# Search for the largest scores in layer 3's attention: four heads at a time on row quarters of TensorE, PSUM banks split four and two

## The chip, the cores and the metric

The kernel runs on one core of a Trainium2 chip. The core has five engines that the profile lists: TensorE (PE for its matmuls, PEld for its weight loads), VectorE (DVE), ScalarE (ACT), GpSimd (POOL) and SyncE (SP, which here only issues transfers). They run side by side, each works through its own queue in order, and semaphores tie them together. Matmuls write to PSUM, which has 8 banks of 512 float32 per partition; VectorE and ScalarE read it from there.

The metric is the device time of one execution, in microseconds (us). The kernel before takes 12436.45 us, the median of three runs (12427.92 to 12447.01).

## The reference

The program is a chain of four layers on a batch of 4 images with 128 channels and 48 x 48 = 2304 positions: a selective-scan block, a deformable convolution, a linear-attention transformer with a mixture of experts, and causal softmax attention with a second mixture of experts. Only the attention of the last layer is touched:

```python
qkv = jnp.einsum('btc,oc->bto', x, qkv_w) + qkv_b
q, k, v = jnp.split(qkv, 3, axis=-1)
q, k, v = (heads(q), heads(k), heads(v))      # 4 heads of 32
scale = 1.0 / np.sqrt(HEAD_DIM)
att = jnp.einsum('bhqd,bhkd->bhqk', q, k) * scale
att = jnp.where(causal, att, -jnp.inf)
att = jax.nn.softmax(att, axis=-1)
out = jnp.einsum('bhqk,bhkd->bhqd', att, v)
out = out.transpose(0, 2, 1, 3).reshape(B, T, C)
return jnp.einsum('btc,oc->bto', out, out_w) + out_b
```

All is float32, x is layer-normalised before it, and the result is added to the stream.

## The kernel before

**Tiling.** An image's 2304 positions are 18 tiles of 128, and 6 blocks (`j`) of three tiles, 384 queries each. The four heads are worked as two pairs (`p`, NP3 = 2). `q` and `k` lie transposed, [128 rows, pair, 2304]: a pair's first head has rows 0 to 31, its second rows 64 to 95. Rows 32 and 96 of `k` hold 1.0, and the same rows of `q` are to receive minus the largest score of each query, so that the score matmul over 64 rows yields score minus maximum and the exponential needs no further pass.

**Two passes over the scores.** The first is the search (`largest`, L2039). For a query tile `i` and a slice `s` of up to 512 keys, one *part* makes the scores of one pair: two matmuls (L2052), one for each head on 64 rows of the array, into the two banks of the tile `sc`. VectorE adds the causal mask in the last slice of a query tile (L2061), reduces over the keys (L2062), and after the last slice takes the maximum over slices (L2065) and writes its negative into `spread` (L2066). When a block's parts are done, `take` turns `spread` by three transposes (L2071) into the tile `ps` and adds it to `q` (L2073). `sc` has one buffer, so a part's matmuls wait for the reduction of the part before.

The second pass goes by *units*, one for each block, pair and key tile `t` up to the diagonal: `scores` (L2105) makes the transposed scores of 128 keys and up to 384 queries for both heads into the two banks of `scT`, ScalarE exponentiates them (L2113) into `pT`, GpSimd zeroes the future on diagonal tiles (L2116), and `weighed` (L2134) multiplies by the values and accumulates into `out`. `scT` has two buffers, so the next unit's scores can be written while the exponential reads the last. There are 4 images x 2 pairs x (3 + 6 + 9 + 12 + 15 + 18) = 504 units, and 4 x 2 x 50 = 400 parts, of which 288 span 512 keys, 32 span 384, 40 span 256 and 40 span 128. A float32 matmul shows in the trace as two matmul and two weight-load records.

**PSUM.** `ps` (projections, transposes and all else) has 1 bank, `sc` 2, `scT` 2 x 2, `out` 1: all 8.

**Order.** The instruction order of each engine is that of the program text. While block `x` = (image, j, p) is worked, the parts of the *following* block (the other pair, or the next j, or the next image) are spread over its units. Other work is popped one step at a time: `others` (normalising, transposing and projecting later blocks and the next image, every second unit, or every unit in blocks under 7 units) and `doing` (dividing by the sums, output projection). `weighed` runs three units behind `scores` (UNIT_LAG). So TensorE's order in a unit is

```python
scores(x, t)
while parts and (total - len(parts)) * max(n - 1, 1) < total * (t + 1):
    parts.pop(0)()
if doing:
    doing.pop(0)()
if others and (t % 2 == 0 or n < 7):
    others.pop(0)()
```

and then `weighed` of an earlier unit. At the end of each block `take` runs. The weights' layout, which puts each head on its rows, is made on the host in `layout`.

Of the kernel before, what the change touches and what calls it, by code (L numbers as in the profile page):

```python
# [15 lines left out]
F32 = mybir.dt.float32  # L16
# [3 lines left out]
AX = mybir.AxisListType  # L20
PSUM = bass.MemoryType.PSUM
DRAM = bass.MemoryType.DRAM

P = 128
NB = 4
C = 128
HW = 48
L = HW * HW
NT = L // P
BLK = 384  # L30
NBLK = L // BLK
G3 = BLK // P
# [33 lines left out]
DH3 = C // NH3  # L66
NP3 = NH3 // 2
# [1840 lines left out]
        _layer3(ctx, env, io, T)  # L1908


UNIT_LAG = 3


def _layer3(ctx, env, io, T):
# [6 lines left out]
    nc, tc, ident = env.nc, env.tc, env.ident  # L1921
    cp = ctx.enter_context(tc.tile_pool(name="l3c", bufs=1))
    bp = ctx.enter_context(tc.tile_pool(name="l3b", bufs=2))
    sp = ctx.enter_context(tc.tile_pool(name="l3s", bufs=2))
    ps = ctx.enter_context(tc.tile_pool(name="l3p", bufs=1, space=PSUM))
    pa = ctx.enter_context(tc.tile_pool(name="l3a", bufs=1, space=PSUM))
    pb = ctx.enter_context(tc.tile_pool(name="l3x", bufs=2, space=PSUM))
    po = ctx.enter_context(tc.tile_pool(name="l3o", bufs=1, space=PSUM))

    def load(name, shape):  # L1930
        t = cp.tile(shape, F32, name=name)
        nc.sync.dma_start(t, io[name])
        return t

    def psum(*shape):
        return ps.tile(list(shape), F32, name="ps", tag="ps")

    w_qk = load("l3_wqk", [P, 2, NP3, P])
    b_qk = load("l3_bqk", [P, 2, NP3])
# [5 lines left out]
    later = load("l3_later", [P, P])  # L1945

    spread = [cp.tile([P, G3, P], F32, name=f"spread{i}") for i in range(NP3)]
# [11 lines left out]
    def normed(im):  # L1959

        t = {}

        def some(g0):
            if g0 == 0:
                t["st"] = sp.tile([P, NT, nc.vector.BN_STATS_DIM], F32, name="st")
                im.mv = sp.tile([P, NT, nc.vector.BN_AGGR_DIM], F32, name="mv")
                im.rstd = sp.tile([P, NT], F32, name="rstd")
                im.q = bp.tile([P, NP3, L], F32, name="q")
                im.k = bp.tile([P, NP3, L], F32, name="k")
            for g in range(g0, g0 + G3):  # L1970
                nc.vector.bn_stats(out=t["st"][:, g, :], in_=im.T[:, g, :])
                nc.vector.bn_aggr(out=im.mv[:, g, :], in_=t["st"][:, g, :])
            if g0 + G3 == NT:
                nc.vector.tensor_scalar_add(im.rstd, im.mv[:, :, 1], 1e-5)
                nc.gpsimd.tensor_tensor(im.rstd, im.rstd, env.half[:, :NT], ALU.pow)

        return [lambda g0=g0: some(g0) for g0 in range(0, NT, G3)]
# [58 lines left out]
            lambda s=s, p=p: project(s, p) for s in range(2) for p in range(NP3)  # L2036
        ] + [value]

    def largest(im, j, p):  # L2039

        neg = spread[p]
        t = {}

        def part(i, s):
            n = (i + 1) * P
            at, end = s * 512, min(s * 512 + 512, n)
            if s == 0:
                t["mx"] = sp.tile([P, 2, 5], F32, name="mx")
            sc = pa.tile([P, 2, 512], F32, name="sc")
            for r in range(2):  # L2050
                rows = slice(r * 64, r * 64 + 64)
                nc.tensor.matmul(  # L2052
                    sc[:, r, : end - at],
                    im.q[rows, p, bass.ts(i, P)],
                    im.k[rows, p, at:end],
                    start=True,
                    stop=True,
                )
            if end == n:
                own = sc[:, :, n - P - at : n - at]  # L2060
                nc.vector.tensor_add(own, own, later.unsqueeze(1).to_broadcast([P, 2, P]))  # L2061
            nc.vector.reduce_max(t["mx"][:, :, s], sc[:, :, : end - at], axis=AX.X)  # L2062
            if end == n:
                top = sp.tile([P, 2], F32, name="top")
                nc.vector.reduce_max(top, t["mx"][:, :, : s + 1], axis=AX.X)  # L2065
                nc.vector.tensor_scalar_mul(neg[:, i - j * G3, DH3 :: 2 * DH3], top, -1.0)  # L2066

        def take():
            pm = psum(P, BLK)
            for g in range(G3):  # L2070
                nc.tensor.transpose(pm[:, bass.ts(g, P)], neg[:, g, :], ident)  # L2071
            at = bass.ts(j, BLK)
            nc.vector.tensor_add(im.q[:, p, at], im.q[:, p, at], pm)  # L2073

        parts = [
            lambda i=i, s=s: part(i, s)
            for i in range(j * G3, (j + 1) * G3)
            for s in range(-(-(i + 1) * P // 512))
        ]
        return parts, take  # L2080

    def output(im, j, oT):
        def project():
# [15 lines left out]
    def scores(x, t):  # L2099
# [3 lines left out]
        for r in range(2):  # L2103
# [7 lines left out]
            )  # L2111
        pT = sp.tile([P, 2, BLK], F32, name="pT", bufs=UNIT_LAG + 2)
        nc.scalar.activation(pT[:, :, cols], sc[:, :, cols], AF.Exp)  # L2113
# [40 lines left out]
    def divide(x):  # L2154
        oT, den = x.im.sums

        def invert(i):
            part = bass.ts(i, BLK // 2)
            nc.vector.reciprocal(den[:, part], den[:, part])
            if i:  # L2160
                nc.vector.tensor_mul(oT, oT, den)

        wait = lambda: None
        return [
            wait,
            wait,
            lambda: invert(0),
            lambda: invert(1),
            wait,
            output(x.im, x.j, oT),  # L2170
        ]
# [5 lines left out]
    images = [Image(b) for b in range(NB)]  # L2177
    blocks = [Block(im, j, p) for im in images for j in range(NBLK) for p in range(NP3)]

    def preparation(im):  # L2180
        return normed(im) + [s for j in range(NBLK) for s in prepare(im, j)]

    def run(steps):
        for s in steps:
            s()

    with tc.manual_schedule(engines=ORDERED):
        pr = psum(1, C)
        nc.tensor.matmul(pr, v_b, oT_w, start=True, stop=True)
        nc.vector.tensor_add(o_b, o_b, pr)  # L2190
        pr = psum(P, C)
        nc.tensor.matmul(pr, env.ones_row, o_b, start=True, stop=True)
        nc.scalar.copy(bias[:, 0, :], pr)
        run(normed(images[0]) + prepare(images[0], 0))
        parts, take = largest(images[0], 0, 0)
        run(parts + [take])
        others = [s for j in range(1, NBLK) for s in prepare(images[0], j)]
        waiting, done, doing = [], [], []
        for i, x in enumerate(blocks):
            n = x.last + 1  # L2200
            if x.j == 0 and x.p == 0 and x.im.b + 1 < NB:
                others += preparation(images[x.im.b + 1])
            following = blocks[i + 1] if i + 1 < len(blocks) else None
            parts, take = largest(following.im, following.j, following.p) if following else ([], None)
            if following and following.im is x.im and x.im.b == 0:

                need = (NBLK - 1 - following.j) * (2 + 2 * NP3 + 1)
                need += 0 if x.im.b + 1 == NB else len(preparation(images[1]))
                while len(others) > need:
                    others.pop(0)()  # L2210
            total = len(parts)
            for t in range(n):
                scores(x, t)
                while parts and (total - len(parts)) * max(n - 1, 1) < total * (t + 1):
                    parts.pop(0)()
                if doing:
                    doing.pop(0)()
                if others and (t % 2 == 0 or n < 7):
                    others.pop(0)()
                waiting.append((x, t))  # L2220
                if len(waiting) > UNIT_LAG:
                    y, s = waiting.pop(0)
                    weighed(y, s)
                    if s == y.last and y.p == NP3 - 1:
                        doing += divide(y)
            run(parts)
            if following and following.im is not x.im:
                run(others)
                others = []
            if take:  # L2230
                take()
        for y, s in waiting:
            weighed(y, s)
            if s == y.last and y.p == NP3 - 1:
                doing += divide(y)
        run(doing)
# [57 lines left out]
def layout(i):  # L2294
# [12 lines left out]
    l3 = {k[8:]: v for k, v in i.items() if k.startswith("L3_attn_")}  # L2307
# [6 lines left out]
    for h in range(NH2):  # L2314
        proj[:, h * DH2 : (h + 1) * DH2, h * NF : (h + 1) * NF] = l2["proj"].transpose(0, 2, 1)

    w_qk = np.zeros((C, 2, NP3, 2, 2, DH3), np.float32)
    w_qk[:, :, :, :, 0] = l3["qkv_w"][: 2 * C].T.reshape(C, 2, NP3, 2, DH3)
    w_qk = w_qk.reshape(C, 2, NP3, P)
    b_qk = np.zeros((2, NP3, 2, 2, DH3), np.float32)  # L2320
    b_qk[:, :, :, 0] = l3["qkv_b"][: 2 * C].reshape(2, NP3, 2, DH3)
    b_qk[1, :, :, 1, 0] = 1.0
    b_qk = b_qk.reshape(2, NP3, P).transpose(2, 0, 1)
    o = {
        "x": i["x"].reshape(NB, C, L),
# [66 lines left out]
```

## Time and profile before

| what | value |
|---|---|
| median of three runs | 12436.45 us |
| profiled execution, its own time | 12545.34 us |
| its span, first to last instruction | 12543.6 us |
| layer 3's attention in it | about 10908 to 12330 us, 1422 us |
| TensorE busy in that stretch | 1288.85 us |
| VectorE busy in that stretch | 708.59 us |
| ScalarE busy in that stretch | 448.01 us |
| mean granted TensorE clock there / over the span | 0.96 / 0.949 |

The profiled execution is 109 us longer than the median of the unprofiled runs. The attention is 11% of the span. "Busy" is the share of time in which an engine shows an instruction; for matmuls the ends are modelled and neighbours overlap, so the distance between the starts of two groups tells more than a busy time. In a timeline line the first column is the start in us, the second how long the merged group shows, `x4` how many records it merges, and what stands in brackets is how long the engine was idle before it and what ended that.

### The profile page before, as it was taken

The numbers are of one execution on the slowest core, as the hardware profiler recorded it, in microseconds if no ns is written. First come the engines' busy times: TensorE is split into PE (matmuls) and PEld (weight loads), VectorE is DVE, ScalarE is ACT, GpSimd is POOL, SyncE is SP. The second block draws the span as 40 slices with busy tenths as digits, with TensorE's granted clock in tenths as the row PEclk, the third lists the DMA queues.
The fourth block names the chain that finished last, engine by engine and source line by source line (L and its number), as shares of the span: only waits on it lengthen the run. The fifth ranks groups of instructions, "written<-read, shape, count | busy, mean of one in ns | idle before, by whom it ended". The sixth has DMA issues, their size and how long they took to land.

```text
span 12543.6 us, 192625 instructions
## 1 busy us (share of the span) xinstructions
PE 10872.6 (87%) x71008; PEld 8365.3 (67%) x71008; DVE 8487.3 (68%) x15484; ACT 6888.6 (55%) x13190; POOL 4409.7 (35%) x4799
## 2 busy tenths in 40 slices
PE   7788787978887787688879999999999999698897
PEld 6667666766676666588857777777777777333333
DVE  6998989888988899544456656566566565455554
ACT  5777767777777777411135655555556555232332
POOL 2433434333333343366633333333333332100001
PEclk9999999999999999899979999999999999799998
DMA  3221222122212222356500000000000000300003
GB/s 122 68 70 63 80 77 71 63 76 80 70 64 76 79 67 67 111 171 177 170 21 2 4 3 3 4 2 4 2 3 5 1 1 12 115 7 8 8 8 126
DMA packets 329879, 677.51 MB, mean 54 GB/s; under 512 B 41556, under 2 KB 152168, under 8 KB 328048
## 3 DMA queue, kind: packets, MB, share of 16 engines
q1 hardware_dynamic: 276064, 493.50, 12.3%
q0 software_dynamic: 51840, 169.91, 4.8%
q8 instruction: 570, 9.34, 0.3%
q14 instruction: 365, 2.99, 0.1%
q10 hardware_dynamic: 1040, 1.77, 0.0%
HBM read 602.63 MB, written 71.85 MB: 54 GB/s over the span
## 4 chain that ended last, share of the span: by engine, by line
PE 43%; DVE 7%; ACT 3%; issue 1%; DMA 1%; POOL 1%; another core or an unknown queue 0%; SPq 0%; ACTq 0%; DVEq 0%; POOLq 0%
PE psum L1466 4%; PE pt L1003 4%; PE psum L1458 4%; PE pc L1352 3%; PE psum L1402 3%; PE scT L2105 3%; PE sc L2052 3%; PE out L2134 3%; PE psum L1372 2%; PE psum L1212 2%; PE psum L1213 2%; PE psum L1146 2%; PE psum L1290 1%; PE psum L1391 1%; DVE mx L1375 1%
## 5 line engine op out<-in xcount | busy, mean ns | idle before, releaser
L576 ACT ACTIVATE hs<-ps,bct 128x256 f32<-128x256 f32 x4608 | 1853.8, 474 | 1174.9 <-PE ps L570 1122.5
L570 PE MATMUL ps<-ident,h 128*128 128x128 f32 x9216 | 1491.9, 294 | 783.4 <-DVE h L556 612.7
L570 PEld LDWEIGHTS ps<-ident,h 128*128 128x128 f32 x9216 | 1079.7, 148 | 1168.7 <-DVE h L556 720.3
L584 PE MATMUL yp<-ident,hs 128*128 128x128 f32 x9216 | 1399.3, 288 | 28.5 <-ACT ys L599 28.5
L516 ACT ACTIVATE dA<-delta,l_Al 128x768 f32<-128x768 f32 x1536 | 1388.2, 936 | 0.3
L523 POOL TENSOR_TENSOR h<-du,rB 128x512 f32<-128x512 f32 x768 | 1077.5, 1403 | 757.9 <-PE ps L570 683.1
L584 PEld LDWEIGHTS yp<-ident,hs 128*128 128x128 f32 x9216 | 1151.2, 150 | 83.6 <-ACT ys L599 57.6
L556 DVE TENSOR_TENSOR_SCAN h<-dA,h 128x256 f32<-128x256 f32 (+1 forms) x1024 | 1084.4, 1059 | 27.3
L556 DVE TENSOR_TENSOR_SCAN h<-dA,carry,h 128x768 f32<-128x768 f32 x512 | 1027.1, 2006 | 10.5 <-ACT dA L516 10.5
L1206 POOL TENSOR_TENSOR T<-T,bias 128x384 f32<-128x384 f32 x384 | 383.7, 999 | 1563.5 <-DVE fn L1134 1523.2
L498 POOL TENSOR_SCALAR_AFFINE_SELECT dB<-bct 128x512 f32<-128x512 f32 x768 | 746.0, 971 | 358.4 <-PE b L530 240.9
L2113 ACT ACTIVATE pT<-scT 128x768 f32<-128x768 f32 (+2 forms) x504 | 377.6, 749 | 841.0 <-PE scT L2105 838.9
L530 PE MATMUL b<-dB,duT 128*128 128x128 f32 x6144 | 828.3, 279 | 0.8 <-ACT duT L456 0.8
L556 DVE TENSOR_TENSOR_SCAN h<-dA,carry,b 128x512 f32<-128x512 f32 x512 | 645.7, 1261 | 263.1 <-PE b L530 242.7
L1003 PE MATMUL pt<-ident,gw 128*128 128x128 f32 x5184 | 685.1, 294 | 147.2 <-DVE gw L997 117.6
L990 POOL DMA_INDIRECT g<-table,idx x648 | 659.9, 1018 | 390.0 <-DVE gw L997 189.6
L530 PEld LDWEIGHTS b<-dB,duT 128*128 128x128 f32 x6144 | 768.6, 196 | 2.4 <-POOL h L523 1.2
L1003 PEld LDWEIGHTS pt<-ident,gw 128*128 128x128 f32 x5184 | 650.1, 207 | 176.9 <-DVE gw L997 110.6
L997 DVE TENSOR_TENSOR gw<-g,wq 128x512 f32<-128x512 f32 x648 | 428.7, 692 | 496.9 <-PE pt L1003 416.7
L563 POOL COPY carry<-h 128x2 f32<-128x2 f32 x512 | 96.8, 189 | 1782.0 <-DVE h L556 1717.7
L2062 DVE TENSOR_REDUCE mx<-sc 128x2 f32<-128x1024 f32 (+3 forms) x400 | 428.3, 1071 | 345.2 <-PE sc L2052 340.2
L527 DVE TENSOR_TENSOR h<-du,rB 128x512 f32<-128x512 f32 x768 | 638.7, 832 | 1.6 <-DMA rB<-rows 1.4
(394 smaller groups left out, 22833.0 us busy)
## 6 DMA issues: line engine op xcount, KB each, us to landing
rB<-rows SPq DMA_DIRECT2D x768, 384.0 KB
w<-f_w SPq DMA_DIRECT2D x64, 1024.0 KB
table<-zero SPq DMA_DIRECT2D x162, 128.0 KB
table<-tok SPq DMA_DIRECT2D x16, 1152.0 KB
g<-table,idx POOLq DMA_INDIRECT x648
yd<-y SPq DMA_DIRECT2D x4, 2304.0 KB
sums<-raw SPq DMA_DIRECT2D x192, 48.0 KB
xb<-x SPq DMA_DIRECT2D x42, 192.0 KB
```

Of the source, the lines that this page charges most:

```text
L498: nc.gpsimd.affine_select(out=x.dB[n], in_=x.bc[:, m0 : m0 + CT // P, n : n + 1].to_broadcast([P, CT // P, P]), pattern=[[0, CT // P], [1, ...
L516: nc.scalar.activation(dA, x.delta[:, d, :], AF.Exp, scale=A[:, d, x.k, n : n + 1])
L523: nc.gpsimd.tensor_mul(h[:, 1, own], x.du[:, 1, own], x.rB[n][:, own])
L527: nc.vector.tensor_mul(x.h[n][:, :, own], x.du[:, :, own], b)
L530: nc.tensor.matmul(b0[:, bass.ts(m, P)], x.duT[:, m, :], x.dB[n][:, m, :], start=True, stop=True,)
L556: nc.vector.tensor_tensor_scan(h, da, b, initial=first, op0=ALU.mult, op1=ALU.add)
L570: nc.tensor.transpose(tt[:, m, bass.ts(d, P)], x.h[n][:, d, bass.ts(2 * q + m, P)], ident)
L576: nc.scalar.activation(hs, tt[:, m, :], AF.Copy, scale=x.bc[:, 2 * q + m, NS + n : NS + n + 1])
L584: nc.tensor.matmul(yp[:, q, (2 * d + m) * P : (2 * d + m + 1) * P], hs[:, bass.ts(d, P)], ident, is_transpose=True, start=n == 0 and m == ...
L990: nc.gpsimd.indirect_dma_start(out=g, out_offset=None, in_=table, in_offset=bass.IndirectOffsetOnAxis(ap=idx[:, j : j + 1], axis=0),)
L1003: nc.tensor.matmul(pt[:, t - t0, :], gw[:, q, :], ident, start=q == 0, stop=q == 3)
L1458: nc.tensor.matmul(pg, y.w["w1"][:, bass.ts(f, P)], t["uT"], start=True, stop=True)
```

## The change

The search takes both pairs, all four heads, in one part. Within a part the four matmuls go to four different quarters of the array's rows: 32 rows each, starting at 0, 64, 32 and 96. For that the second pair's heads move in the weights' layout from rows 0 and 64 to rows 32 and 96, and its extra rows (the 1.0 in `k`, minus the maximum in `q`) to 0 and 64. A part writes four PSUM banks, so `sc` becomes [128, 2, 2, 512], and `scT` keeps one buffer of two banks. Mask, reduction and maximum work on four heads in one instruction; the negation is still one instruction for each pair. The search runs for the next `j` and is spread over the units of both pairs of the present one; both pairs' `take` run one after the other at the end of the second pair's block.

```diff
+KW = 512
...
-    pb = ctx.enter_context(tc.tile_pool(name="l3x", bufs=2, space=PSUM))
+    pb = ctx.enter_context(tc.tile_pool(name="l3x", bufs=1, space=PSUM))
...
-    def largest(im, j, p):
+    def largest(im, j):
...
-            sc = pa.tile([P, 2, 512], F32, name="sc")
-            for r in range(2):
-                rows = slice(r * 64, r * 64 + 64)
-                nc.tensor.matmul(
-                    sc[:, r, : end - at],
...
+            sc = pa.tile([P, 2, NP3, KW], F32, name="sc")
+            for p in range(NP3):
+                for r in range(2):
+                    r0 = r * 64 + p * DH3
+                    rows = slice(r0, r0 + DH3)
+                    nc.tensor.matmul(
+                        sc[:, r, p, : end - at],
+                        im.q[rows, p, bass.ts(i, P)],
+                        im.k[rows, p, at:end],
+                        start=True,
+                        stop=True,
+                    )
             if end == n:
-                own = sc[:, :, n - P - at : n - at]
-                nc.vector.tensor_add(own, own, later.unsqueeze(1).to_broadcast([P, 2, P]))
-            nc.vector.reduce_max(t["mx"][:, :, s], sc[:, :, : end - at], axis=AX.X)
+                own = sc[:, :, :, n - P - at : n - at]
+                mask = later.unsqueeze(1).unsqueeze(1).to_broadcast([P, 2, NP3, P])
+                nc.vector.tensor_add(own, own, mask)
+            nc.vector.reduce_max(t["mx"][:, :, :, s], sc[:, :, :, : end - at], axis=AX.X)
             if end == n:
-                top = sp.tile([P, 2], F32, name="top")
-                nc.vector.reduce_max(top, t["mx"][:, :, : s + 1], axis=AX.X)
-                nc.vector.tensor_scalar_mul(neg[:, i - j * G3, DH3 :: 2 * DH3], top, -1.0)
+                top = sp.tile([P, 2, NP3], F32, name="top")
+                nc.vector.reduce_max(top, t["mx"][:, :, :, : s + 1], axis=AX.X)
+                for p in range(NP3):
+                    neg = spread[p][:, i - j * G3, (1 - p) * DH3 :: 2 * DH3]
+                    nc.vector.tensor_scalar_mul(neg, top[:, :, p], -1.0)
...
-        return parts, take
+        return parts, lambda: [take(p) for p in range(NP3)]
...
-            following = blocks[i + 1] if i + 1 < len(blocks) else None
-            parts, take = largest(following.im, following.j, following.p) if following else ([], None)
...
+            following = blocks[i + NP3] if i + NP3 < len(blocks) else None
+            if x.p == 0:
+                parts, take = largest(following.im, following.j) if following else ([], None)
+                total, units = len(parts), 0
...
-                while parts and (total - len(parts)) * max(n - 1, 1) < total * (t + 1):
+                units += 1
+                while parts and (total - len(parts)) * (NP3 * n - 1) < total * units:
                     parts.pop(0)()
...
-            if take:
-                take()
+            if x.p == NP3 - 1:
+                run(parts)
...
+                if take:
+                    take()
```

More of the change, by code (lines that the diff above doesn't have):

```diff
@@ L2037, in prepare @@
         ] + [value]
-    def largest(im, j, p):
-        neg = spread[p]
+    def largest(im, j):
         t = {}
@@ L2045, in part @@
             n = (i + 1) * P
-            at, end = s * 512, min(s * 512 + 512, n)
+            at, end = s * KW, min(s * KW + KW, n)
             if s == 0:
-                t["mx"] = sp.tile([P, 2, 5], F32, name="mx")
-            sc = pa.tile([P, 2, 512], F32, name="sc")
-            for r in range(2):
-                rows = slice(r * 64, r * 64 + 64)
-                nc.tensor.matmul(
-                    sc[:, r, : end - at],
[L2054 to L2058, printed above, removed]
+                t["mx"] = sp.tile([P, 2, NP3, -(-L // KW)], F32, name="mx")
@@ L2063, in part @@
             if end == n:
-                top = sp.tile([P, 2], F32, name="top")
-                nc.vector.reduce_max(top, t["mx"][:, :, : s + 1], axis=AX.X)
-                nc.vector.tensor_scalar_mul(neg[:, i - j * G3, DH3 :: 2 * DH3], top, -1.0)
-        def take():
+                top = sp.tile([P, 2, NP3], F32, name="top")
[3 more added lines that the diff above has]
+                    nc.vector.tensor_scalar_mul(neg, top[:, :, p], -1.0)
@@ L2069, in take @@
+        def take(p):
             pm = psum(P, BLK)
             for g in range(G3):
-                nc.tensor.transpose(pm[:, bass.ts(g, P)], neg[:, g, :], ident)
+                nc.tensor.transpose(pm[:, bass.ts(g, P)], spread[p][:, g, :], ident)
             at = bass.ts(j, BLK)
@@ L2077, in largest @@
             for i in range(j * G3, (j + 1) * G3)
-            for s in range(-(-(i + 1) * P // 512))
+            for s in range(-(-(i + 1) * P // KW))
         ]
-        return parts, take
+        return parts, lambda: [take(p) for p in range(NP3)]
     def output(im, j, oT):
@@ L2194, in _layer3 @@
         run(normed(images[0]) + prepare(images[0], 0))
-        parts, take = largest(images[0], 0, 0)
+        parts, take = largest(images[0], 0)
         run(parts + [take])
@@ L2202, in _layer3 @@
                 others += preparation(images[x.im.b + 1])
-            following = blocks[i + 1] if i + 1 < len(blocks) else None
-            parts, take = largest(following.im, following.j, following.p) if following else ([], None)
[L2205 to L2211, printed above, removed]
+            following = blocks[i + NP3] if i + NP3 < len(blocks) else None
+            if x.p == 0:
+                parts, take = largest(following.im, following.j) if following else ([], None)
+                total, units = len(parts), 0
+                if following and following.im is x.im and x.im.b == 0:
+                    need = (NBLK - 1 - following.j) * (2 + 2 * NP3 + 1)
+                    need += 0 if x.im.b + 1 == NB else len(preparation(images[1]))
+                    while len(others) > need:
+                        others.pop(0)()
             for t in range(n):
                 scores(x, t)
-                while parts and (total - len(parts)) * max(n - 1, 1) < total * (t + 1):
+                units += 1
+                while parts and (total - len(parts)) * (NP3 * n - 1) < total * units:
                     parts.pop(0)()
@@ L2225, in _layer3 @@
                         doing += divide(y)
[L2226 to L2229, printed above, removed]
-            if take:
-                take()
+            if x.p == NP3 - 1:
+                run(parts)
+                if following and following.im is not x.im:
+                    run(others)
+                    others = []
+                if take:
+                    take()
         for y, s in waiting:
@@ L2317, in layout @@
     w_qk = np.zeros((C, 2, NP3, 2, 2, DH3), np.float32)
-    w_qk[:, :, :, :, 0] = l3["qkv_w"][: 2 * C].T.reshape(C, 2, NP3, 2, DH3)
+    wide = l3["qkv_w"][: 2 * C].T.reshape(C, 2, NP3, 2, DH3)
+    for p in range(NP3):
+        w_qk[:, :, p, :, p] = wide[:, :, p]
     w_qk = w_qk.reshape(C, 2, NP3, P)
     b_qk = np.zeros((2, NP3, 2, 2, DH3), np.float32)
-    b_qk[:, :, :, 0] = l3["qkv_b"][: 2 * C].reshape(2, NP3, 2, DH3)
-    b_qk[1, :, :, 1, 0] = 1.0
+    for p in range(NP3):
+        b_qk[:, p, :, p] = l3["qkv_b"][: 2 * C].reshape(2, NP3, 2, DH3)[:, p]
+        b_qk[1, p, :, 1 - p, 0] = 1.0
     b_qk = b_qk.reshape(2, NP3, P).transpose(2, 0, 1)
```

## The prediction, made before the changed kernel had run

> **What bounds the kernel now.** I read the page's slices first, to find where the changed code runs, then the busy times of that stretch, its instructions by line and shape, its waits, and last the timeline of single units.
>
> ```profile
> PE   7788787978887787688879999999999999698897
> ...
> DVE  6998989888988899544456656566566565455554
> ```
>
> Each digit is a fortieth, 314 us. Layer 3's attention starts late in slice 35 and ends early in slice 40; in the four between, PE is at 8 to 9 tenths and DVE at 5.
>
> ```profile
> 10908.00:12330.00 1422.00, 1288.85 (x6308) 494.98 (x6306) 708.59 (x1198) 448.01 (x646) 91.51 (x170) 0.96 0.03 7
> ```
>
> Columns: stretch, length, busy PE, PEld, DVE, ACT, POOL, clock. PE is busy 91% of 1422 us, DVE 50%, ACT 32%: PE's order sets the time. By line and shape, same stretch:
>
> ```profile
> L2105 PE MATMUL scT<-q,k 64*128 64x384 f32 x1632 | 379.0, 541 | 45.1 <-DVE q L2073 45.1
> ...
> L2062 DVE TENSOR_REDUCE mx<-sc 128x2 f32<-128x1024 f32 x288 | 352.9, 1225 | 341.3 <-PE sc L2052 340.2
> L2113 ACT ACTIVATE pT<-scT 128x768 f32<-128x768 f32 x408 | 330.5, 810 | 683.5 <-PE scT L2105 681.3 <-PE sc L2052 1.3 <-POOL T L2000 0.6
> L2052 PE MATMUL sc<-k,q 64*128 64x512 f32 x1152 | 315.7, 623 | 34.2 <-DVE mx L2062 32.8
> ```
>
> The search is 316 us of PE at this shape alone. Two steady units, the first with a part and the second without:
>
> ```profile
> 11574.44 0.87 PE L2134 MATMUL out<-pT,v 128*64 128x384 f32 x4
> ...
> 11575.24 0.92 PE L2105 MATMUL scT<-q,k 64*128 64x384 f32 x4
> ...
> 11575.99 1.02 PE L2052 MATMUL sc<-k,q 64*128 64x512 f32 x4
> ...
> 11576.26 0.81 ACT L2113 ACTIVATE pT<-scT 128x768 f32<-128x768 f32 x1 [1.69 <-PE scT L2105]
> ...
> 11576.94 0.87 PE L2134 MATMUL out<-pT,v 128*64 128x384 f32 x4
> ```
>
> ```profile
> 12306.06 0.87 PE L2134 MATMUL out<-pT,v 128*64 128x384 f32 x4
> 12306.24 0.81 ACT L2113 ACTIVATE pT<-scT 128x768 f32<-128x768 f32 x1 [1.03 <-PE scT L2105]
> 12306.85 0.30 PEld L2105 LDWEIGHTS scT<-q,k 64*128 64x128 f32 x4 [0.60 <-issue]
> ...
> 12307.70 0.87 PE L2134 MATMUL out<-pT,v 128*64 128x384 f32 x4
> ```
>
> A unit with a 512-key part takes 11576.94 - 11574.44 = 2.50 us, one without 12307.70 - 12306.06 = 1.64 us. So a full part costs PE 0.86 us, though it holds four records of 0.43 us of streaming: the two heads run at once on the two halves of the rows. By the same scale (keys / 512) a part costs 0.64, 0.43 and 0.22 us for 384, 256 and 128 keys.
>
> **The change part by part.**
>
> *Search matmuls.* Before: 288 x 0.86 + 32 x 0.64 + 40 x 0.43 + 40 x 0.22 = 294 us of PE. After there are 200 parts: 144, 16, 20 and 20 of these sizes, each with twice the heads. Whether four row quarters run at once is not in this trace. The nearest row is four column quarters, in the experts:
>
> ```profile
> 12452.08 1.06 PE L1781 MATMUL psum<-w,pooled 128*32 128x512 f32 x8
> ...
> 12453.08 1.06 PE L1789 MATMUL psum<-b,ident 64*32 64x512 f32 x8
> ```
>
> Eight records, four matmuls of 512, take 12453.08 - 12452.08 = 1.00 us, against 0.95 us for the two of L2052 (11576.94 - 11575.99). So quarters can run four at a time, at least across columns. Around it I add what a change of array layout costs: the score matmuls (64 rows) and the search (32 rows) no longer share one. The 384-column scores take 0.75 us (11575.99 - 11575.24) where they are followed by the same layout and 12307.70 - 12306.85 = 0.85 us where a change follows: 0.10 us. The first weight load after a change is not hidden: scT's 0.75 us is 0.11 above its streaming of 0.64. So a full part after costs 0.86 + 0.10 + 0.11 + 0.01 = 1.08 us, and 0.86, 0.65 and 0.44 for the smaller ones. Sum: 144 x 1.08 + 16 x 0.86 + 20 x 0.65 + 20 x 0.44 = 191 us. **Saved: 103 us.** Bounds: at best the change of layout costs nothing (147 us of PE, 147 saved); at worst the quarters run two by two, 1.93 us per full part, 336 us, 42 lost. I take the best-case streaming because both packed rows in the trace, halves by rows and quarters by columns, run fully side by side.
>
> The Trainium skill, "TensorE: Matmul & The Clock Gate", section "Measured speedup vs the span model", gives 3.07 times rather than 4 for four row tiles of 32 at 512 columns; by that a full part's streaming would be an estimated 4 x 0.85 / 3.07 = 1.11 us instead of 0.85 us, and the saving some 60 us instead of 103. No run here shows row quarters yet.
>
> *One scores tile.* With two buffers PE may write unit t+1's scores while ACT reads unit t's. With one, from scT's first matmul to the exponential's start is 11576.26 - 11575.24 = 1.02 us, the exponential is 0.81, and PE's next load starts 0.05 us after ACT's end (the copy of L2144 ends at 12304.36, the load that waits for it starts at 12304.42): 1.88 us from scores to scores. A unit with a part (2.50, after 2.72) covers it; so does one with a projection (a unit with one and a part is 3.34, so 0.84 us more). A unit with neither rises from 1.64 to 1.88. Counting the program's order after the change: 197 of 504 units carry a part (3 parts run ahead of the first), 81 of the rest carry a matmul of other work, 226 carry nothing. **Lost: 226 x 0.24 = 54 us.** Bounds: nothing, if the load goes ahead of the wait and ACT is sooner (0.11 less); 504 x 0.24 = 121 if every unit pays.
>
> The Trainium skill speaks against this edit: "Perfetto Trace Analysis", section "Optimizing Tensor Performance", Matmuls, has independent groups rotate through banks so that evacuation overlaps the next group. Breaking it costs, by the rows, the 1.88 us above; the trace before agrees with the rule in that, with two buffers, no load of scT waits over 0.6 us on the exponential.
>
> *Block ends.* `take` costs PE, from its transposes to the next scores, 1.20 us in a long block (transposes at 11901.98, scores at 11903.18: three transposes, then 0.55 of L2073 on DVE). 48 of them are 58 us. After there are 24 double ones: the second set of transposes waits for the bank `ps` until the first add is done, then 0.43 more, 1.63 us: 39 us. **Saved: 19 us.** Bounds: nothing to 48 x 2. The last part of a block now falls two or more units before the end in all but the shortest blocks, so DVE's chain behind it (mask, reduction, maximum, two negations) lies beside units.
>
> *DVE.* Rows of the reduction are 1.23 us for 1024 elements, 0.69 for 512: 1.04 ns each. 2048 take 2.29 us. Total falls by 200 x 0.16 us of start-up; a mask of 512 elements is 0.43 + 0.27 = 0.70. DVE is at 50%, so this gives nothing by itself. What counts is `sc`, still one buffer: a part can follow the last after 1.08 + 0.12 + 2.29 + 0.05 = 3.54 us, 0.7 more with a mask. Units with parts mostly alternate with units without, 2.72 + 1.88 = 4.60 us, which covers it; about 8 times an image parts stand in adjacent units and lose some 1.1 us: 35 us. Before, PE waited 56.6 us for it:
>
> ```profile
> PE sc L2052 <- DVE mx L2062: 56.6, 58, 1.9
> ...
> PE scT L2105 <- DVE q L2073: 45.1, 47, 4.1
> ```
>
> (the 110.7 us shown on PEld for the same releaser are loads that idle while PE streams). **Saved: 20 us.** Behind a 2.29 us reduction in DVE's queue wait q's evacuation (L2015), the divisions and the `take` adds, and PE's projections wait for `ps` behind these; bounds 40 lost to 57 saved.
>
> *The start.* Ahead of the first unit three parts now serve four heads with nothing beside them: DVE has 256 more elements in each mask (0.27 us), 256, 512 and 768 more in the reductions (0.27, 0.53, 0.80) and one more negation each (0.18): **3 us lost.** Weights and biases move inside the same tensors; the same transfers, POOL and SP instructions are issued: nothing.
>
> Sum: 103 - 54 + 19 + 20 - 3 = 85 us saved. It is made against the profiled execution (span 12543.6, its own time 12545.34); the median is 109 us below that. 85 us off the median gives 12351 us.
>
> **The rivals.**
>
> *Row quarters go two by two* (slower). PE then pays 1.93 us for a full part: 336 - 191 = 145 us more, 60 lost in all, 12496 us. It decides from a full part of 1.58 us on: 85 of the 145 us are 0.59 of the way from 1.08 to 1.93. For it: four row quarters write four whole banks at once, and the widest thing the trace shows is two; against it: both packed rows run without loss. Chance 0.15.
>
> *They overlap in part*, halfway between: 72 us more, 13 saved, 12423 us. The skill's 3.07 lies on this side. Chance 0.08.
>
> *Every unit pays the single scores tile*, because ACT's other evacuations (0.48 to 0.58 us each) or late masks stand ahead of the exponential: 121 instead of 54, 18 saved, 12418 us. ACT's 32% speaks against it. Chance 0.05.
>
> *DVE's longer reductions hold up `ps` and `take`* in the short blocks of each image, where PE already waits (1.9 and 4.1 us at most in the rows above): 30 lost instead of 20 saved, 35 saved, 12401 us. Chance 0.10.
>
> **How the numbers follow.** The forecast, 12351 us, has 0.62; its own range, from the ends of the wait and block-end terms, is 12290 to 12400. About 0.2%, 25 us, is what a measurement of this kernel can tell from no change (its three runs span 19 us). Faster: 0.62 + 0.10 = 0.72; same: 0.08 + 0.05 = 0.13; slower: 0.15. The range leaves out the slower rival and 0.05 below, and reaches over the halfway case: 12290 to 12430.
>
> **What would show it.** The eight records of a full part, 32 rows by 512, in about 1.0 us would bear out the first term; 1.8 us, the slower rival. Scores to scores of 1.88 us in units without a part, ended by the exponential, bears out the second. Twenty-four pairs of `take`, and PE waits on the reduction of about 35 us, the others. The prediction is wrong if the stretch between the first search matmul and the last value matmul does not fall from 1422 to about 1337 us, or if the granted clock (0.85 in the first 80 us of the third image, 1.00 after) falls because of the new gaps.

## The result and the profile after

The changed kernel takes 12300.35 us, the median of four runs (12287.92 to 12312.93), against 12433.08 us for the kernel before, with a fourth run added to its three: a ratio of 0.9894, 95% interval 0.9881 to 0.9906. That is 133 us, 1.06%, less; 85 us were forecast, and 12300 us lies inside the stated range of 12290 to 12430. A second set of runs of the same kernel, on another chip, gave 0.9906 (0.9889 to 0.9922).

The profiled execution (its own time 12295.53 us) is 250 us shorter than that of before, far more than the medians say. 108 us of that are layer 1, which the change does not touch: its span was 5240 to 6275 us before and 5239 to 6168 us here, and in the changed kernel's second profile 5240 to 6292 us again. Layer 3's attention is what remains. From its first instruction to its first score matmul it takes 54.5 us (37.7 before), from there to the last value matmul 1256.8 us (1411.4 before): 138 us less in all, which agrees with the medians. The page of the changed kernel, the same two rows as before:

```profile
PE   7778788977888787789979999999999999689997
...
DVE  6998889888888889755455655655665665455553
```

The digits hardly move: TensorE is still at 9 tenths in the stage, which is now shorter. The stretch from the first score matmul to the last value matmul (columns: stretch, length, busy PE, PEld, DVE, ACT, POOL, clock, DMA share, GB/s):

```profile
10823.50:12080.30 1256.80, 1142.58 (x6259) 401.49 (x6258) 637.50 (x832) 444.62 (x641) 90.24 (x169) 0.98 0.03 8
```

By line and shape in the same stretch:

```profile
L2111 PE MATMUL scT<-q,k 64*128 64x384 f32 x1632 | 379.0, 542 | 38.3 <-ACT pT L2119 38.1
...
L2066 DVE TENSOR_REDUCE mx<-sc 128x4 f32<-128x2048 f32 x144 | 329.9, 2291 | 216.3 <-PE sc L2055 215.6
L2055 PE MATMUL sc<-k,q 32*128 32x512 f32 x1152 | 172.0, 667 | 14.8 <-DVE mx L2066 14.3
```

The search's matmuls at the full shape fell from 315.7 to 172.0 us of busy time with the same number of records, 1152: four now lie beside each other where two did. The reduction takes 2291 ns, forecast 2.29 us. The score matmuls wait for the exponential where they waited for `q` before. A full part, up to the value matmuls behind it, and, from another place, an empty unit, from its scores to the next:

```profile
11861.23 1.14 PE L2055 MATMUL sc<-k,q 32*128 32x512 f32 x8
...
11862.30 0.20 PEld L2140 LDWEIGHTS out<-pT,v 128*64 128x64 f32 x4 [0.76 <-issue]
```

```profile
11754.63 0.92 PE L2111 MATMUL scT<-q,k 64*128 64x384 f32 x4 [0.17 <-ACT pT L2119]
...
11755.66 0.81 ACT L2119 ACTIVATE pT<-scT 128x768 f32<-128x768 f32 x1 [1.07 <-PE scT L2111]
11756.52 0.30 PEld L2111 LDWEIGHTS scT<-q,k 64*128 64x128 f32 x4 [0.84 <-ACT pT L2119]
```

A full part takes 11862.30 - 11861.23 = 1.07 us (forecast 1.08), and an empty unit 11756.52 - 11754.63 = 1.89 us (forecast 1.88), ended by the exponential. Both prices of the prediction's mechanism are there to a hundredth. The slope agrees: from 128 to 512 keys a part on quarters grows from 0.43 to 1.07 us and one on halves from 0.32 to 0.95, the same 0.64 us, with twice the heads.

To see where the rest came from I took the start of the first score matmul of each of the 504 units from the trace and set the rows' prices against what the program puts into the unit: scores 0.21 us + columns / 600, values 0.15 + columns / 600, a part keys / 600 plus 0.01 (0.225 on quarters), three transposes 0.55, a projection 0.84, a value or output step 0.86. What a unit lasts beyond that is counted as a wait: for the exponential, where scores to scores cannot be shorter; at a block's end, in the unit that `take` follows (its transposes are counted there); or any other. The prices are those at the full clock, so what matmuls lose at half clock stands among the waits too. So these are figures of this accounting and not times of the trace, and a few us go one way or the other with the prices taken. All in us, from the first score to the last value matmul:

| | before | changed | one scores tile | order only | halves |
|---|---|---|---|---|---|
| scores and values | 763 | 763 | 763 | 763 | 763 |
| parts of the search | 294 | 189 | 294 | 293 | 293 |
| other matmuls | 122 | 123 | 122 | 123 | 123 |
| wait for the exponential | 0 | 56 | 22 | 0 | 55 |
| block ends | 103 | 54 | 100 | 54 | 54 |
| other waits | 129 | 72 | 127 | 140 | 67 |
| sum | 1411 | 1257 | 1428 | 1374 | 1356 |
| ahead of the first score | 38 | 55 | 38 | 59 | 57 |

So by this accounting 105 us came from the search's matmuls, 56 went to the single scores tile, 49 came from the block ends, 57 from other waits, and 17 went to the start. The last three columns are experiments.

### The profile page after: what moved, and what is told of

Same layout as the page of the kernel before. It is cut to its first block, busy times and chain, and to the rows that moved or that the text cites. A ratio compares the mean times of both kernels' runs of the same rounds, so it can differ in the third digit from the quotient of the medians.

```text
span 12293.8 us, 192110 instructions
## 1 busy us (share of the span) xinstructions
PE 10700.3 (87%) x71008; PEld 8228.4 (67%) x71008; DVE 8434.0 (69%) x15140; ACT 6893.9 (56%) x13190; POOL 4463.2 (36%) x4799
## 4 chain that ended last, share of the span: by engine, by line
PE 37%; DVE 6%; ACT 4%; DMA 3%; POOL 3%; issue 3%; SPq 0%; ACTq 0%; DVEq 0%; POOLq 0%
PE psum L1466 4%; PE psum L1458 4%; PE pc L1352 3%; PE psum L1402 3%; PE scT L2111 3%; PE psum L1372 2%; POOL g L990 2%; PE psum L1212 2%; DMA g<-table,idx 2%; PE psum L1213 2%; PE psum L1146 2%; PE out L2140 2%; PE sc L2055 2%; PE psum L1290 1%; ACT pT L2119 1%
## 5 line engine op out<-in xcount | busy, mean ns | idle before, releaser
L990 POOL DMA_INDIRECT g<-table,idx x648 | 705.1, 1088 | 242.1 <-issue 139.7
L1003 PEld LDWEIGHTS pt<-ident,gw 128*128 128x128 f32 x5184 | 608.7, 193 | 146.8 <-DVE gw L997 113.4
L1219 ACT ACTIVATE wksq<-psum,l_cols 128x384 f32<-128x384 f32 x192 | 111.6, 581 | 788.3 <-DVE wk L1217 788.3
```

Source lines behind the costliest of these rows:

```text
L990: nc.gpsimd.indirect_dma_start(out=g, out_offset=None, in_=table, in_offset=bass.IndirectOffsetOnAxis(ap=idx[:, j : j + 1], axis=0),)
L1003: nc.tensor.matmul(pt[:, t - t0, :], gw[:, q, :], ident, start=q == 0, stop=q == 3)
```

## The experiments

Each set has its own runs of the kernel before on the same chip (12530.3 us in the first set of four, 12547.38 us in the second), so ratios are compared, not times; the times in the expectations are for the first chip.

**One scores tile, on the kernel before.**

```diff
-    pb = ctx.enter_context(tc.tile_pool(name="l3x", bufs=2, space=PSUM))
+    pb = ctx.enter_context(tc.tile_pool(name="l3x", bufs=1, space=PSUM))
```

> The kernel before with one change: the scores tile has one buffer instead of two (the two banks that come free are left unused). Search, order and everything else as before. My theory: only units that carry neither a part of the search nor a matmul of other work pay, 1.88 us instead of 1.64. By the program's order before, 110 of the 504 units are such, so 110 x 0.24 = 26 us slower than before, about 12460 us, and the 1.64 us units show 1.88 to 1.89. Rival: every unit pays the wait for the exponential: 504 x 0.24 = 121 us slower. Third: the wait is covered by the units' lag: no difference.

Measured: ratio 1.0019 (1.0010 to 1.0029), 24 us slower; first score to last value 1428 us, 16 more. Its timeline in the last block:

```profile
12305.58 0.30 PEld L2105 LDWEIGHTS scT<-q,k 64*128 64x128 f32 x4 [0.84 <-ACT pT L2113]
...
12306.60 0.81 ACT L2113 ACTIVATE pT<-scT 128x768 f32<-128x768 f32 x1 [1.07 <-PE scT L2105]
12307.47 0.30 PEld L2105 LDWEIGHTS scT<-q,k 64*128 64x128 f32 x4 [0.84 <-ACT pT L2113]
```

Scores to scores, 12307.47 - 12305.58 = 1.89 us. The 24 us, and the 22 in the table's row of waits for the exponential, are near the 26 us of the first theory, by which only the empty units pay; every unit paying would have been 121 us.

**The order alone, on the kernel before.** The loop is the changed kernel's, and this stands in for its `largest`:

```diff
+    def both_pairs(im, j):
+        (parts0, take0), (parts1, take1) = [largest(im, j, p) for p in range(NP3)]
+        parts = [part for pair in zip(parts0, parts1) for part in pair]
+        return parts, lambda: [take0(), take1()]
```

> The kernel before with the new order alone: the search for both pairs of the next j is spread over the units of both pairs of this j, and the two takes run one after the other at the end of the second pair's block. A part is still one pair on halves of the rows, the search tile has two banks, the scores tile two buffers. My theory now: the changed kernel's trace has 48 us less at block ends and 57 us less in other waits than the kernel before. The block ends belong to the order, so 48 us come here too; if the other waits also belong to the order, 105 us faster than before (about 12328 us), if they belong to the parts of four heads, 48 us faster (about 12385 us). Rival, the prediction's own figure for the block ends: 19 us faster (about 12414 us).

Measured: ratio 0.9996 (0.9986 to 1.0006), no difference that these runs can tell; the profiled executions show 15 us less, which the interval allows. None of the three figures was met, though the block ends did what the theory said: 54 us in the table, 49 less than before. Two things took it back. 22 us are lost ahead of the first score, in part because the preparation of the second block, which ran inside image 0's first block, now runs before it (that block falls from 44.2 to 36.5 us). And the other waits rise from 129 to 140 us. Its waits on the search tile (columns: total us, times, longest), where the kernel before has 110.7 and 56.6 us:

```profile
PEld sc L2052 <- DVE mx L2062: 121.9, 180, 2.9
...
PE sc L2052 <- DVE mx L2062: 79.0, 74, 1.9
```

With the parts of both pairs spread together, 40 units carry two or more parts (28 before), and the second waits for the reduction of the first. So the 57 us of other waits do not belong to the order.

**Halves in place of quarters, on the changed kernel.**

```diff
-                    r0 = r * 64 + p * DH3
-                    rows = slice(r0, r0 + DH3)
+                    rows = slice(r * 64, r * 64 + 64)
```

> The changed kernel, with the four matmuls of a part on 64 rows each, two after two, as before, instead of on four quarters of 32 rows (the rows added hold zeros in the queries, so the scores are the same). Four banks, one scores tile, order and merged reductions stay. My theory: a full part costs 1.72 us of PE again instead of 1.07, all parts 294 us instead of 189, so 105 us slower than the changed kernel, about 12405 us. Rival: the gain lies in the order and the merged reductions, PE is not what binds, and the quarters give 30 us or less: 12330 us or below.

Measured: ratio 0.9975 (0.9965 to 0.9984), against 0.9894 of the changed kernel: 0.81%, 101 us slower than it (86 us against its second ratio, 0.9906; the changed kernel itself was not run in this set). The stretch is 1356 us, 99 more, and in the table the parts alone differ by 104. The rival falls: TensorE binds, and the quarters are worth all that their matmuls save. Halves also keep the low "other waits" (67 us) of the changed kernel with the old price of the matmuls. Against the order alone, with 140, what differs is the merged parts (four heads to one mask, one reduction, one maximum, never two parts in a unit) and the single scores tile, which by the first experiment moves these waits by 2 us. So the merged parts took the 57 us away, and neither the order nor the quarters did.

**The reduction cut short, on both kernels.** The maximum is taken over the first 64 keys of each slice only.

```diff
-            nc.vector.reduce_max(t["mx"][:, :, :, s], sc[:, :, :, : end - at], axis=AX.X)
+            nc.vector.reduce_max(t["mx"][:, :, :, s], sc[:, :, :, :64], axis=AX.X)
```

> The changed kernel with the reduction cut to the first 64 keys of each slice: the maximum over the other keys is left out, so this is a probe of VectorE's time and no solution. A full part's reduction falls from 2.29 us to about 0.43. My theory: what is left of TensorE's waits outside the block ends (71 us) is for the greater part the search tile's single buffer, so about 35 us go, and 3 to 5 us at the block ends. Rival: they are waits on divisions, statistics, copies to the sums and the projections' one bank: less than 10 us go.

> The kernel before with the reduction cut to the first 64 keys of each slice: the maximum over the other keys is left out, a probe of VectorE's time. A full part's reduction falls from 1.23 us to about 0.3. My theory: the 57 us of waits that the change took away were waits for this reduction, in units that carry two parts or a part right behind another, so about 60 us or more of the 129 go here. Rival: they came from the order and the other VectorE work: less than 25 us go.

Measured from one execution of each, so there is no interval: 12342.32 us from the changed kernel, 66 less than its profiled execution in this set (12408.27), and 12457.67 us from the kernel before, 90 less than its median. In the changed kernel the other waits fall to 16 us, from 72 in its first profile and 74 in the second, and the block ends from 54 to 52; its reductions are now

```profile
L2066 DVE TENSOR_REDUCE mx<-sc 128x4 f32<-128x256 f32 x197 | 83.7, 425 | 332.6 <-PE sc L2055 330.2
```

425 ns instead of 2291. On the kernel before the other waits fall from 129 to 50, the block ends from 103 to 89. TensorE's own waits for the reduction, 110.7 and 56.6 us there, become

```profile
PEld sc L2052 <- DVE mx L2062: 26.6, 21, 2.0
...
PE sc L2052 <- DVE mx L2062: 21.5, 35, 1.0
```

So the greater part of the other waits hangs on the reduction in both kernels: 74 - 16 = 58 us of them in the changed one, 129 - 50 = 79 in the one before, with what comes back in clock. I expected 35 and 60 or more. The length of the reduction thus accounts for 79 - 58 = 21 us of the 55 that lie between the two kernels here (129 against 74). The other 34 (50 against 16) stay when the reduction is short: masks, maxima and the round trips of twice as many parts, 28 units with several of them, and time at half clock (below). These runs do not tell these apart.

**More scores banks where no part is live, and `take` on two tiles.** First version, on the changed kernel (its `scores` takes the search tile's first banks where `spare` is set):

```diff
+                units += 1
+                due = parts and (total - len(parts)) * (NP3 * n - 1) < total * units
+                since = 0 if due else since + 1
+                spare = since > 1 and not spare
+                scores(x, t, spare)
...
+        if spare:
+            sc = pa.tile([P, 2, NP3, KW], F32, name="sc")[:, :, 0, :]
+        else:
+            sc = pb.tile([P, 2, 512], F32, name="scT")
```

and both pairs' transposes in one search tile, `pm[:, 0, p, :]`.

> The changed kernel with two additions. The scores use two of the search tile's four banks in every second unit where no part stands in this unit or the one before it (163 units change banks, 124 of them among the 226 that carry nothing else); and both pairs' transposes at a block's end go to banks of the search tile instead of the one bank that the first add must free. My theory: 124 x 0.25 = 31 us for the first, 24 x 0.5 = 12 us for the second: 43 us faster than the changed kernel, about 12257 us. Rival: the wait only moves to the search, whose parts must now wait for an exponential: no gain, 12300 us.

Measured: ratio 0.9877 (0.9860 to 0.9893); the stretch is 1237 us, 20 less than the changed kernel's where 43 were expected. The last blocks gave what they should (69.2 to 62.1 us in the second and third image), the second blocks lost (42.2 to 45.0), and the block ends hardly moved. Both pairs' transposes wrote one tile, and the second set waited for the first add:

```profile
11737.97 0.55 DVE L2080 TENSOR_TENSOR q<-q,sc 128x384 f32<-128x384 f32 x1 [1.76 <-PE sc L2079]
11738.58 0.31 PEld L2079 LDWEIGHTS sc<-ident,spread 128*128 128x128 f32 x3 [0.89 <-DVE q L2080]
11738.58 0.55 PE L2079 MATMUL sc<-ident,spread 128*128 128x128 f32 x3 [0.65 <-DVE q L2080]
```

The second set still starts 0.06 us after the first add has ended (11738.52), though they use different banks. The second version, which lends banks in the last blocks only and puts the transposes into two tiles, mends both:

```diff
-                spare = since > 1 and not spare
+                spare = x.j == NBLK - 1 and since > 1 and not spare
...
+            pms = [psum(P, BLK), pa.tile([P, 2, NP3, KW], F32, name="sc")[:, 0, 0, :BLK]]
```

> The changed kernel once more, on the chip of this set, so that the version below can be set against it. Expected: 0.9894 of the kernel before, as measured first, within 0.15%.

> The changed kernel with the two additions of the version before, mended where its trace showed a loss. The scores use two of the search tile's banks in every second unit only in the last block of each image (j = 5), and not in the shorter ones, where they waited for a reduction. At a block's end the first pair's transposes go to the bank they had, the second pair's to the search tile, two tiles instead of one, so that the second set need not wait for the first add. My theory: the last blocks give 34 us in first-to-last units as in the version before (4.7, 7.1, 7.1 and 8.5 us an image), which is 27 to 31 us after image 0, and 24 block ends give 0.5 us each, 12 us: some 40 us faster than the changed kernel. Rival: the adds still stand between, because the scores wait for both pairs' queries: 28 us faster and no more.

Measured in one set: the changed kernel 12425.71 us, ratio 0.9906 (0.9889 to 0.9922); this version 12372.46 us, ratio 0.9866 (0.9850 to 0.9883): 53 us less in the medians, 37 us less from first score to last value matmul (1221.8 against 1258.9). The two profiled executions differ by 39 us; the other 14 are within the scatter of the runs (the changed kernel's span 28 us). So the theory's 40 us were about met. The last blocks are 61.8 and 61.6 us in the second and third image and gave 28 us in all four, where the expectation's own four figures add up to 27 and not to its 34; the block ends are 43 us in place of 55. A block end of the changed kernel, and one of this version:

```profile
11650.29 0.55 PE L2077 MATMUL ps<-ident,spread 128*128 128x128 f32 x3
...
11651.48 0.55 PE L2077 MATMUL ps<-ident,spread 128*128 128x128 f32 x3 [0.65 <-DVE q L2079]
...
11651.96 0.92 PE L2111 MATMUL scT<-q,k 64*128 64x384 f32 x4
```

```profile
11740.31 0.55 PE L2079 MATMUL ps<-ident,spread 128*128 128x128 f32 x3
...
11740.70 0.49 PE L2079 MATMUL sc<-ident,spread 128*128 128x128 f32 x3
...
11741.60 0.92 PE L2115 MATMUL scT<-q,k 64*128 64x384 f32 x4 [0.41 <-DVE q L2080]
```

From the first transposes to the next scores, 1.67 us becomes 1.29. Of the versions that take the maximum over all keys this one has the lowest ratio, clear of the kernel before and of the changed one; from the first version (0.9877) the ratios do not tell it apart, only the stretch does (1222 against 1237 us).

## Why the prediction was right, point by point

The direction, the mechanism and the two largest terms held. The sum was 48 us short: the gains at the block ends and in the waits were sized too low by 30 and 37 us, the loss at the start by 14. That the time still fell inside the range is in part luck: it lies 10 us from the range's lower end, and without the 14 us unforeseen at the start it would have been below. The stretch from the first search matmul to the last value matmul, for which 1337 us were forecast, fell from 1421 to 1283 us.

- *Search matmuls*, 103 us forecast: 105 in the table. The best-case streaming, taken from halves by rows and quarters by columns, was the right choice. The halves experiment shows it by undoing it alone: 99 us of the stretch. The rivals in which the quarters run two by two, or overlap halfway, are out.
- The Trainium skill's 3.07 times ("TensorE: Matmul & The Clock Gate", "Measured speedup vs the span model") would, by the prediction's estimate, have saved some 60 us. Here a full part on quarters takes 1.07 us, of which 0.21 are the change of layout and its load, and 0.86 streaming, as for halves: for the streaming the measurement decides for 4. Counted with the 0.21, it is an estimated 4 x 0.86 / 1.07 = 3.2 times.
- *One scores tile*, 54 us lost: 56 in the table, 1.89 us for an empty unit against 1.88. The rival in which every unit pays is out; on the kernel before the edit cost 24 us.
- *Block ends*, 19 us saved: 49 in the table. The double end of a long block was right (1.63 forecast, 1.67 in the lines above), the number of ends too. What failed is that one long block's price was taken for all: 1.20 us for each of the 48 ends before, while their mean is 103 / 48 = 2.1, and 1.63 for each of the 24 after, while their mean is 54 / 24 = 2.25. So both sums were too low, 58 against 103 us and 39 against 54. In the first blocks of an image the ends before come to 36 us for 8 of them, because `take` there stands behind statistics and reductions in VectorE's queue. One of them in the kernel before:

```profile
11684.54 0.68 PE L2071 MATMUL ps<-ident,spread 128*128 128x128 f32 x3
11689.35 1.65 PE L2105 MATMUL scT<-q,k 64*128 64x384 f32 x4 [4.13 <-DVE q L2073]
```

  The add that the scores wait for starts at 11688.66 only, when VectorE has done with a reciprocal and image statistics.
- *DVE*, 20 us saved: 57 in the table. The reduction's length is worth 21 of these, as the probes show, and that this is the forecast's 20 is luck: the shortened reduction takes 79 us of waits away before and 58 after, where 56.6 and 35 stood in the sum, both too low by about 23. The other 34 were not in the sum at all. The step that failed is the reading of the wait rows: I counted TensorE's 56.6 us alone and put all of the 110.7 us of its loads down to loads that idle beside streaming. With the short reduction on the kernel before, the 56.6 us fall by 35 only, but the other waits by 79. After the change the two rows are

```profile
PEld sc L2055 <- DVE mx L2066: 29.6, 34, 1.7
PE sc L2055 <- DVE mx L2066: 25.0, 27, 2.6
```

  and both fell. I had also counted only adjacent units in the order after, and not the 28 units before that carry several parts, where each part pays its whole round trip through VectorE inside the unit. The rival in which longer reductions hold up `ps` and `take` is out: the waits fell in all blocks but the fifth (8.4 to 9.0 us).
- *The start*, 3 us lost: 17 measured. I missed a step that is moved: the loop that forces preparation ahead now looks a whole block on, so the second block's transposes and projections run before the first score matmul. They take 12.4 us there, from 10811.11 to 10823.51. Image 0's first block is 18 us shorter, where the first blocks of the next two images are 5 to 6 us shorter; with the order alone it is 8 us shorter. How much of the 18 is the moved step is not shown: its time at half clock fell too, from 44 to 13 us.
- The granted clock did not fall because of the new gaps: its mean from the first search matmul to the last value matmul is 0.97, and was 0.96.

## What to carry to other kernels

Take prices of packed matmuls from packed rows of the same trace, and add what a change of array layout costs, here 0.10 us and 0.11 us for the load that is not hidden: here that gave the price of an unseen shape to 0.01 us. A second buffer is worth only what the units without cover would wait, so count these units in the program's order, and lend them banks that are idle in that stretch. Where a stage has short and long blocks, price a block end from both kinds, and read how many round trips to another engine stand in one unit before calling a wait hidden.

## What the runs showed of the hardware that was not expected

Four float32 matmuls on four row quarters, each writing a whole PSUM bank, stream in the time that two take on halves, 0.86 us. From their start to the value matmuls it is 1.07 us, against 0.95 us for the two, which follow score matmuls of their own layout.

The granted clock in the stretch is either 0.5 or 1.0 in the trace's records, never between. That agrees with the two states that the Trainium skill describes ("TensorE: Matmul & The Clock Gate", Part 1). Its time at 0.5 is 108 us before and 57 after (64 in the second profile). With the reduction cut short it is 34 us on the kernel before and 18 on the changed one. It does not follow the waits alone: with the order alone it is 49 us, though the other waits are the highest of the table. In the kernel before, nearly all of it lies in the first two blocks of the images. At 0.5 a group of score matmuls shows 1.65 us (11689.35 above) where it shows 0.92 at 1.0. So part of what a wait costs here may come back as matmuls at half speed after it. The first two blocks of the third image, before and after:

```profile
11658.72:11739.21 80.49, 60.28 (x274) 25.73 (x275) 47.73 (x115) 16.96 (x28) 10.09 (x15) 0.85 0.04 11
```

```profile
11475.61:11543.25 67.64, 54.64 (x292) 20.97 (x291) 48.73 (x95) 16.96 (x28) 10.12 (x15) 0.87 0.05 12
```

80 us at a mean clock of 0.85 became 68 us at 0.87. How much of the 34 us left open above is this was not measured. If all of the time at 0.5 were matmuls at half speed, it would cost half of itself: an estimated 54 us before and 29 after, and 17 and 9 with the short reductions, so at most 17 of the 34 us.
